# A four-layer decoder kernel: the last layer's experts in groups of four, and layer 2's causal masks added on TensorE

## The chip, the cores and the metric

The kernel runs on one core of one Trainium2 chip. The metric is the device time of one execution in microseconds (us), taken as the median over runs; lower is better. The core has five engines with queues of their own that meet through semaphores: TensorE (PE, matrix products into PSUM; its weight loads are shown as PEld), VectorE (DVE), ScalarE (ACT), GpSimd (POOL) and SyncE (SP), which in this kernel issues nearly all DMAs.

## The reference, cut to what matters

Four layers work one after the other on x of shape (4, 512, 128), each as self-attention, cross-attention to a context of 154 rows, and a feed-forward part, each followed by a residual and a layer norm. Two of the twelve parts matter here. The causal attention of layer 2 has 16 heads of 64, and keys and values are one projection; the last layer's feed-forward part is a mixture of one shared and seven routed experts with 352 inner values each.

```python
# layer 2, attention: a key after its query is masked; scale 1/sqrt(128), keys times 1 + k_weights
logits = jnp.where(mask, logits, jnp.asarray(-1000000.0, logits.dtype))
a = jax.nn.softmax(logits, axis=-1)
y = jnp.einsum("bhij,bhjv->bhiv", a, kv)          # then y @ w_o

# last layer, feed-forward
def _expert(x, wg, wu, wd):
    return jax.nn.silu(x @ wg) * (x @ wu) @ wd
shared_out = _expert(x, shared_gate, shared_up, shared_down)
probs = jax.nn.sigmoid(x @ Wr * routing_bias)
scores, idx = jax.lax.top_k(probs, TOPK)          # TOPK = 2
scores = scores / scores.sum(-1, keepdims=True)
for e in range(n_exp):                            # 7 routed experts
    combined = combined + _expert(xf, routed_gate[e], routed_up[e], routed_down[e]) * weights[:, e:e + 1]
return shared_out + combined.reshape(b, s, d)
```

Every expert is computed for every row, and the two chosen ones get a weight that isn't zero.

## The kernel before

The twelve parts are Python generators that emit instructions piece by piece. The order on each engine is the order in which the pieces are emitted, written out by hand; the scheduler does not reorder. A part has a first phase, which is interleaved with the end of the part before it by a pattern of letters (ORDER), a main phase, and a tail. An Agenda holds small pieces that are due at a given step (normalising a finished batch, routing the next). The work goes batch by batch, 512 rows at a time, kept transposed (features on the 128 partitions) as `xT`.

**Layer 2's attention (`l2_attn`, with the class `Causal`).** A unit is one batch and two heads; there are 4 x 8 = 32. Heads lie in partitions 0 to 63 and 64 to 127. The scores of a unit are a triangle of query tiles of 128: query tile qt meets qt + 1 key tiles. They are computed in three parts, `PARTS`: part 0 is query tile 3 (512 keys), part 1 is query tiles 2 and 0 (384 and 128 keys), part 2 is query tile 1 (256 keys), each for both heads. `scores` (L1137) puts the scores in a PSUM buffer `scc`. `maxima` (L1153) runs one custom DVE instruction for each query tile and head, which adds the bf16 mask tile `cmaskb`, turns the sign, writes the scores back to PSUM, and gives the negative maximum. `exps` (L1161) runs the exponential on ACT with that maximum as bias and also sums the rows; `norm` divides, with the reciprocal on DVE (L1167) and the product on POOL (L1170). `turned` (L1186) transposes the probabilities of the unit on PE into `ptc`, which ACT or DVE copies out (L1522, L1533, L1547), and `products` (L1199) multiplies by the values.

`step(i)` of `l2_attn` interleaves three units: queries and keys of unit i + 2 (`psqk`, L1471) and its values (`psv`, transposes of the keys, L1481), scores of unit i + 1, transposes and products of unit i, and the output projection of unit i - 1 (`ypo`, L1492). Eight times a step a PSUM buffer of two banks is taken, from a ring of three in fixed turn: scores 0, transposes 0, queries and keys, scores 1, transposes 1, scores 2, values, transposes 2. Each of these must wait until the one three turns earlier has been read. When a projection for the next part of the layer (`ps_proj`, L400) comes between, the turn moves on by one. Layer 1's feed-forward part uses the same class.

**The last layer's experts (`l3_ffn`).** For each batch and expert there are three chunks of inner values: 128, 128 and 96. `gated` (L1935) makes two products, gate and up, into a pair of PSUM banks `psgu` (or `psguy` and `psguv`), ACT makes the silu (L1937), and DVE the product into the tile `hT` (L1938). `down` (L1946) multiplies the three chunks of an expert by its down weights, into `ype`, and DVE adds it, with the routing weight, to `ys` (L1952, L1958). `chunk(q)` issues chunk q, and behind every second chunk of an expert the down product of the expert before it:

```python
            if c == 1 and q > NCH:
                before = q // NCH - 1
                down(*divmod(before, NE))
```

There are 4 batches x 8 experts x 3 chunks = 96 chunks. After the last one comes the last down product, then the layer norm of the last batch and its store.

The functions that the change touches, with the line numbers of the profile:

Of the kernel before, what the change touches and what calls it, by code (L numbers as in the profile page):

```python
# [21 lines left out]
P = 128  # L22
# [62 lines left out]
    return out.reshape(P, P)  # L85


def _rope_tables():
    freq = np.exp(np.arange(0, D, 2, dtype=np.float32) * np.float32(-np.log(10000.0) / D))
    ang = np.arange(S, dtype=np.float32)[:, None] * freq[None, :]  # L90
    return _fold(np.cos(ang).astype(np.float32)), _fold(np.sin(ang).astype(np.float32))


def _layer_params(name, p):

    if name == "L0_attn":
        cos, sin = _rope_tables()
        return dict(
            cos=cos, sin=sin,
            wq=_heads(p["Wq"].T), wk=_heads(p["Wk"].T), bq=_head_bias(p["bq"]), bk=_head_bias(p["bk"]),  # L100
            wv=p["Wv"].T, bv=_rows(p["bv"]), wo=p["Wo"].T, bo=_rows(p["bo"]),
        )
    if name.endswith("xattn"):
        out = dict(wq=_heads(p["Wq"].T), wk=_heads(p["Wk"].T), wv=p["Wv"].T)
        if "bq" in p:
            out |= dict(bq=_head_bias(p["bq"]), bk=_head_bias(p["bk"]), bv=_rows(p["bv"]))
        if "Wo" in p:
            out |= dict(wo=p["Wo"].T)
        if "bo" in p:
            out |= dict(bo=_rows(p["bo"]))  # L110
        if "gamma" in p:
            out |= dict(gamma=_rows(p["gamma"]), beta=_rows(p["beta"]))
        return out
    if name == "L0_ffn":
        return dict(
            w1=p["w1_w"].T, w2=p["w2_w"].T, s1=_cols(p["w1_s"]), s2=_cols(p["w2_s"]),
            h1=_fold(p["h1_w"].T), h1s=_cols(p["h1_s"]), h2=_fold(p["h2_w"].T), h2s=_cols(p["h2_s"]),
            w3=_fold(p["w3_w"].T), s3=_rows(p["w3_s"]),
        )
    if name == "L1_attn":  # L120
        wx = np.zeros((2 * P, P), np.float32)
        for at in (0, 64, 96):
            wx[:, at : at + 32] = p["W_x"][:, 8:]
        wx[:, 32:40] = p["W_x"][:, :8]
        wdt = np.zeros((P, 2 * P), np.float32)
        wdt[32:40] = p["W_dt"]
        return dict(
            w_in=p["W_in"], cwr=_rows(p["conv_w"].T), cb=_cols(p["conv_b"]), wx=_fold(wx), wdt=wdt,
            bdt=_cols(p["b_dt"]), alog=_fold(p["A_log"]), dd=_cols(p["D"]), wout=_fold(p["W_out"]),
        )  # L130
    if name == "L1_ffn":
        ve = p["value_experts"].transpose(2, 1, 0, 3).reshape(P, -1)
        oe = p["output_experts"].reshape(8, 4, 2, 64, P).transpose(2, 3, 1, 0, 4).reshape(P, -1)
        return dict(wq=p["w_q"], wk=p["w_k"], wg=p["w_gate"], ve=ve, oe=oe)
    if name in ("L1_ffn", "L2_attn"):
        return dict(wq=p["w_q"], wkv=p["w_kv"], kw=_cols(p["k_weights"]), wo=_fold(p["w_o"]))
    if name == "L2_ffn":
        return dict(
            dwk=p["dw_kernel"].reshape(P, 3), dwb=_cols(p["dw_bias"]), pw=p["pw_w"].T, pwb=_cols(p["pw_b"]),
            rw=p["router_w"].T, rb=_rows(p["router_b"]),  # L140
            ew=p["expert_w"].transpose(2, 0, 1).reshape(P, -1), eb=_rows(p["expert_b"]),
            ow=p["out_w"].T, ob=_rows(p["out_b"]), nw=_rows(p["norm_w"]),
            dn=p["ff_down_w"].T, dnb=_tall(p["ff_down_b"].reshape(-1, 1)), up=_tall(p["ff_up_w"].T),
            upb=_rows(p["ff_up_b"]),
        )
    if name == "L3_attn":
        return dict(
            wd=p["W_down"], wq=_heads(_block_diag(p["toqueries"])), wk=_heads(_block_diag(p["tokeys"])),
            wv=_block_diag(p["tovalues"]), wo=p["W_unify"], bo=_rows(p["b_unify"]),
        )  # L150
    if name == "L3_ffn":
        gate = np.concatenate([p["shared_gate"][None], p["routed_gate"]]).transpose(1, 0, 2).reshape(P, -1)
        up = np.concatenate([p["shared_up"][None], p["routed_up"]]).transpose(1, 0, 2).reshape(P, -1)
        dn = np.concatenate([p["shared_down"][None], p["routed_down"]])
        full = np.zeros((8, 3 * P, P), dn.dtype)
        full[:, : dn.shape[1]] = dn
        dn = full.reshape(8, 3, P, P).transpose(2, 0, 1, 3).reshape(P, -1)
        return dict(wr=p["Wr"], rb=_rows(p["routing_bias"]), gate=gate, up=up, dn=dn)
    raise KeyError(name)
# [15 lines left out]
def decoder_kernel(ctx: ExitStack, tc: tile.TileContext, x, ctxT, mask1, mask3, packs, offsets, out, layers):  # L175
# [936 lines left out]
    class Causal:  # L1112
# [4 lines left out]
        KEYS = (((0, 0),), ((1, 0), (3, 384)), ((2, 0),))  # L1117
        WIDTH = (512, 512, 256)

        def __init__(self, pool, room):  # L1120
            self.ap, self.room, self.work = pool, room, None

            self.mask = pool.tile([P, S], BF16, name="cmaskb", bufs=1)
            nc.gpsimd.memset(self.mask[:, : S - P], 0.0)
            make_causal_mask(nc, self.mask[:, S - P :], MASKED)
            self.nm = {}
            self.pr = {}
            self.pT = {}

        def scores(self, u, part, q, k):  # L1130

            sc = psum2("scc")
            for i, (qt, at) in enumerate(self.PARTS[part]):
                n = (qt + 1) * P
                for r in range(2):
                    rows = slice(64 * r, 64 * r + 64)
                    nc.tensor.matmul(  # L1137
                        sc[:, r, at : at + n], lhsT=q[rows, qt * P : n], rhs=k[rows, :n], start=(i == 0), stop=True,
                        skip_group_check=True,
                    )  # L1140
            nt = len(self.PARTS[part])
            nm = small.tile([P, 2, 2], F32, tag=f"nm{part}", name="nm")
            zs = small.tile([P, 2, 2], F32, tag=f"zs{part}", name="zs")
# [3 lines left out]
            def maxima():  # L1147

                for i, (qt, at) in enumerate(self.PARTS[part]):
                    n = (qt + 1) * P  # L1150
                    for r in range(2):
                        of = sc[:, r, at : at + n]
                        nc.vector.tensor_tensor_reduce(  # L1153
# [3 lines left out]
            def exps():  # L1157
                for i, (qt, at) in enumerate(self.PARTS[part]):
                    to = at + (qt + 1) * P
                    for r in range(2):  # L1160
                        nc.scalar.activation(  # L1161
                            pr[:, r, at:to], sc[:, r, at:to], AF.Exp, bias=nm[:, i, r : r + 1], scale=-1.0,
                            accum_out=zs[:, i, r : r + 1],
                        )

# [39 lines left out]
    def l1_ffn(w, cur, new, last, room):  # L1205
        NH, NE, DH, NC = 8, 8, 64, 4
        units = B * NC
        keep, pool = room.take("keep"), room.take("early")
        causal = Causal(pool, room)
        made, gates, yTs, oTs, gTs, waiting = {}, {}, {}, {}, {}, []  # L1210
        agenda = Agenda()
        state_x, state_T = cur["x"], cur["xT"]
# [240 lines left out]
    def l2_attn(w, cur, new, last, room):  # L1453
# [4 lines left out]

        nc.vector.tensor_scalar(kw1, w["kw"], 1.0, D ** -0.5, ALU.add, ALU.mult)
        wo = w["wo"].rearrange("p (c d) -> p c d", c=NC)  # L1460
        causal = Causal(pool, room)
        made, ypo, oTs = {}, {}, {}
        agenda = Agenda()
        state_x, state_T = cur["x"], cur["xT"]
# [420 lines left out]

    def l3_ffn(w, cur, new, last, room):

        NE, HID, NCH = 8, 352, 3
        keep = room.take("keep")
        dn = w["dn"].rearrange("p (e c d) -> p e c d", e=NE, c=NCH)  # L1890
        xs, xT = cur["x"], cur["xT"]
        weight, hidden, ys_of = {}, {}, {}
        agenda = Agenda()

        def routed(b):
# [31 lines left out]
        def gated(b, e, c):  # L1927
            src = xT[:, b, :]
            if c == 0:
                hidden[b, e] = keep.tile([P, NCH, S], F32, tag="hT", name="hT")  # L1930
            n = min(P, HID - c * P)
            at = e * HID + c * P
            ps = psum_pair("psgu")
            for r, wt in enumerate((w["gate"], w["up"])):
                nc.tensor.matmul(ps[r][:n], lhsT=wt[:, at : at + n], rhs=src, start=True, stop=True)  # L1935
            sg = keep.tile([P, S], F32, tag="sg", name="sg")
            nc.scalar.activation(sg[:n], ps[0][:n], AF.Silu)  # L1937
            nc.vector.tensor_tensor(hidden[b, e][:n, c, :], sg[:n], ps[1][:n], ALU.mult)  # L1938

        def down(b, e):  # L1940
            hT = hidden.pop((b, e))
            yp = psum_a("ype")
            for t in range(NT):
                for c in range(NCH):
                    n = min(P, HID - c * P)
                    nc.tensor.matmul(  # L1946
                        yp[:, t * P : (t + 1) * P], lhsT=hT[:n, c, t * P : (t + 1) * P], rhs=dn[:n, e, c, :],
                        start=(c == 0), stop=(c == NCH - 1),
                    )
            if e == 0:  # L1950
# [6 lines left out]
            for t in range(NT):  # L1957
                nc.vector.scalar_tensor_tensor(  # L1958
                    ys[:, t, :], yp[:, t * P : (t + 1) * P], weight[b][:, t, e - 1 : e], ys[:, t, :], ALU.mult, ALU.add
                )  # L1960

        def chunk(q):
            b, r = divmod(q, NE * NCH)
            e, c = divmod(r, NCH)
            if q < steps:
                gated(b, e, c)
            if c == 1 and q > NCH:
                before = q // NCH - 1
                down(*divmod(before, NE))
                if before % NE == NE - 1:  # L1970
                    agenda.add(q + 1, finish_pieces(before // NE, ys_of.pop(before // NE), new, last, split=True))
            agenda.run(q)

        steps = B * NE * NCH
        gated(0, 0, 0)
        yield PIECE
        routed(0)
# [6 lines left out]
                yield PIECE  # L1984
        yield READY
        for b in range(1, B):
            agenda.add(b * NE * NCH - 8, [lambda b=b: routed(b), lambda b=b: chosen(b)])
        for q in range(6, steps + 1):
            chunk(q)
            yield PIECE  # L1990
# [421 lines left out]
```

## Time and profile before

| | us |
|---|---|
| median of 3 runs | 2703.14 |
| lowest and highest | 2700.03, 2704.36 |
| the profiled execution, whole | 2705.39 |
| its span, first to last instruction | 2703.4 |

| engine | busy us | share of the span |
|---|---|---|
| PE | 2410.7 | 89% |
| PEld (weight loads, overlap PE) | 1161.6 | 43% |
| DVE | 1754.2 | 65% |
| ACT | 1247.0 | 46% |
| POOL | 1056.1 | 39% |

Layer 2's attention has its main phase from about 1452 to 1851 us of the span, the last layer's experts from about 2433 us to the end. In the profile's rows a group is given as line, engine, operation, output and inputs with the program's names, shapes (partitions x elements, or for PE rows x columns of the weights, then the moving operand), count, and busy time and mean duration. A row of a timeline begins with the start and the time until the group's end; what stands in brackets is the idle time before it and what released it. A matmul with f32 operands shows as two records, so counts of f32 matmuls are twice those in the code. The ends of matmuls are modelled, and neighbours seem to overlap by some hundredths of a microsecond; distances between starts are the safer measure.

### The profile page before, as it was taken

How to read it: one execution, taken by the hardware profiler on the slowest of the kernel's cores; microseconds unless marked ns; L12 is line 12 of the kernel's file. 1: busy time of each engine (PE TensorE's matmuls, PEld its weight loads, DVE VectorE, ACT ScalarE, POOL GpSimd, SP SyncE). 2: the span in 40 equal slices, each digit the busy share in tenths (PEclk: the TensorE clock that was granted, in tenths of full speed). 3: DMA queues.
4: the chain of work that ended last, by engine and by line, in shares of the span. 5: the costliest groups of instructions: out<-in, count | busy, mean ns of one | idle time of the engine just before them, and what ended most of it. 6: DMA issues, size and time to landing. Idle time of an engine off the chain costs nothing.

```text
span 2703.4 us, 37772 instructions
## 1 busy us (share of the span) xinstructions
PE 2410.7 (89%) x13974; PEld 1161.6 (43%) x13994; DVE 1754.2 (65%) x3484; ACT 1247.0 (46%) x2525; POOL 1056.1 (39%) x1376
## 2 busy tenths in 40 slices
PE   5898889978877989999999999997988999999998
PEld 1233334433334434444444555554455233446665
DVE  6796951288896665555556666666756887664444
ACT  3676432377652434333333455453543787443221
POOL 2342520166675336556542444443445343310000
PEclk9998999989998999999999999998998999999999
DMA  5421310000002400000000000002102241400000
GB/s 152 119 79 57 101 35 0 0 0 0 0 16 80 142 7 1 0 1 1 1 1 1 15 12 1 13 13 83 39 1 59 77 115 23 139 24 1 4 5 8
DMA packets 75560, 96.39 MB, mean 36 GB/s; under 512 B 23664, under 2 KB 62320, under 8 KB 75376
## 3 DMA queue, kind: packets, MB, share of 16 engines
q1 hardware_dynamic: 74224, 92.14, 11.7%
q8 instruction: 110, 1.80, 0.3%
q10 hardware_dynamic: 1152, 1.84, 0.2%
q14 instruction: 74, 0.61, 0.1%
HBM read 63.92 MB, written 33.49 MB: 36 GB/s over the span
## 4 chain that ended last, share of the span: by engine, by line
PE 62%; DVE 16%; ACT 9%; POOL 5%; issue 4%; DMA 2%; SPq 1%; POOLq 0%; DVEq 0%; ACTq 0%
PE psgu L1935 4%; PE psve L1289 4%; PE av L709 4%; PE yT L1332 3%; PE scc L1137 3%; PE ype L1946 3%; ACT pr L1161 3%; PE psh L1624 3%; DVE scc L1153 3%; PE avc L1199 3%; PE ptc L1186 3%; DVE top L967 2%; PE sc L670 2%; PE avx L995 2%; DVE top L674 2%
## 5 line engine op out<-in xcount | busy, mean ns | idle before, releaser
L1170 POOL TENSOR_TENSOR pr<-pr,zs 128x1024 f32<-128x1024 f32 x192 | 237.4, 1254 | 246.6 <-DVE zs L1167 232.4
L674 DVE TENSOR_REDUCE top<-sc 128x2 f32<-128x1024 f32 x256 | 300.8, 1216 | 46.8 <-PE sc L670 43.0
L695 ACT ACTIVATE pT<-st 128x512 f32<-128x512 f32 x512 | 276.1, 597 | 89.0 <-PE st L686 85.8
L1161 ACT ACTIVATE pr<-scc,nm 128x256 f32<-128x256 f32 (+3 forms) x384 | 199.0, 530 | 198.2 <-DVE zs L1167 78.3
L1153 DVE CUSTOM_DVE_ANT_0 scc<-scc,cmaskb 128x256 f32<-128x256 f32 (+3 forms) x384 | 191.5, 499 | 131.4 <-PE scc L1137 112.6
L967 DVE TENSOR_REDUCE top<-scx 128x4 f32<-128x616 f32 x256 | 192.1, 794 | 88.1 <-PE scx L954 77.2
L973 ACT ACTIVATE pTx<-stx 128x512 f32<-128x512 f32 x256 | 139.3, 596 | 202.8 <-PE scx L954 135.5
L2143 POOL TENSOR_TENSOR hh<-hh,cs 128x1024 f32<-128x1024 f32 x64 | 149.4, 2355 | 74.0 <-DVE hh L2139 50.1
L709 PE MATMUL av<-pT,vbuf 128*32 128x256 f32 x2048 | 162.8, 393 | 8.4 <-ACT avs L509 8.4
L492 POOL CAST nmP<-top 128x16 bf16<-128x16 f32 x96 | 25.6, 267 | 363.7 <-DVE top L967 202.5
L1294 DVE TENSOR_TENSOR vtmp<-psve,gm 128x1024 f32<-128x1024 f32 x64 | 78.3, 1224 | 133.2 <-PE psve L1289 133.1
L337 POOL TENSOR_TENSOR rsf<-mvf,eps 128x4 f32<-128x4 f32 x48 | 9.9, 206 | 393.7 <-DVE mvf L335 392.6
L1137 PE MATMUL scc<-k,q 64*128 64x512 f32 (+3 forms) x768 | 142.5, 469 | 10.8 <-ACT pr L1161 6.2
L1186 PE MATMUL ptc<-ident,pr 128*128 128x128 f32 x960 | 138.4, 282 | 10.3 <-ACT pT L1533 5.7
L2139 DVE TENSOR_TENSOR_SCAN hh<-da,pb 128x1024 f32<-128x1024 f32 x64 | 142.6, 2270 | 0.0
L1289 PE MATMUL psve<-w_L_ffn,xT 128*128 128x512 f32 x256 | 125.7, 615 | 17.4 <-ACT pr L1161 11.9
L670 PE MATMUL sc<-kP,qP 64*128 64x512 bf16 x512 | 106.3, 414 | 35.1 <-DMA qP<-far_q 16.6
L1299 POOL TENSOR_TENSOR vtmp<-vtmp 128x512 f32<-128x512 f32 x60 | 76.0, 1267 | 153.9 <-DVE vtmp L1294 133.6
L2152 PE MATMUL acc<-hh,ident 128*128 128x512 f32 x256 | 132.5, 644 | 3.1 <-DVE yt L2161 1.9
L1199 PE MATMUL avc<-pT,v 128*64 128x512 f32 (+3 forms) x768 | 131.2, 449 | 0.8 <-DVE pT L1522 0.5
L1186 PEld LDWEIGHTS ptc<-ident,pr 128*128 128x128 f32 x960 | 103.4, 141 | 55.1 <-issue 13.9
L1332 PE MATMUL yT<-gT,w_L_ffn 128*128 128x512 f32 x256 | 122.9, 603 | 0.0
(418 smaller groups left out, 5044.4 us busy)
## 6 DMA issues: line engine op xcount, KB each, us to landing
qP<-far_q SPq DMA_DIRECT2D x24, 768.0 KB, 6.3
w_L_ffn<-in_L_ffn SPq DMA_DIRECT2D x24, 512.0 KB, 6.5
far_q<-part SPq DMA_DIRECT2D x44, 192.0 KB, 2.8
qP<-far_q SPq DMA_DIRECT2D x24, 256.0 KB, 4.1
far_q<-part SPq DMA_DIRECT2D x44, 128.0 KB, 2.4
kP<-far_k SPq DMA_DIRECT2D x7, 768.0 KB, 5.3
kP<-far_kc SPq DMA_DIRECT2D x16, 231.0 KB, 4.5
w_L_attn<-in_L_attn SPq DMA_DIRECT2D x6, 512.0 KB, 6.6
```

What stands on the lines that cost most here:

```text
L674: return lambda: nc.vector.tensor_reduce(top[:, qt, 2 * gp : 2 * gp + 2], sc, AX.X, ALU.max, negate=True)
L695: nc.scalar.activation(pT, st, AF.Exp)
L709: nc.tensor.matmul(m["av"][32 * g : 32 * g + 32, part], lhsT=m["v"][:, kt, 4 * j + g, :], rhs=weights_of[s, g][:, part], start=(kt == 0 an ...
L967: nc.vector.tensor_reduce(ops.maxima(a)[:, 2 * qp : 2 * qp + 2, 2 * gp : 2 * gp + 2].rearrange("p i r -> p r i"), sc, AX.X, ALU.max, negat ...
L1137: nc.tensor.matmul(sc[:, r, at : at + n], lhsT=q[rows, qt * P : n], rhs=k[rows, :n], start=(i == 0), stop=True, skip_group_check=True,)
L1153: nc.vector.tensor_tensor_reduce(of, of, self.mask[:, S - n :], -1.0, 3.0e38, ALU.add, ALU.min, nm[:, i, r : r + 1])
L1161: nc.scalar.activation(pr[:, r, at:to], sc[:, r, at:to], AF.Exp, bias=nm[:, i, r : r + 1], scale=-1.0, accum_out=zs[:, i, r : r + 1],)
L1170: nc.gpsimd.tensor_tensor(pr[:, :, at : at + n], pr[:, :, at : at + n], zs[:, i, :, None].to_broadcast([P, 2, n]), ALU.mult)
L1186: nc.tensor.transpose(pt[:, r, to : to + P], self.pr[u, p][:, r, lo : lo + P], ident)
L1199: nc.tensor.matmul(av[64 * r : 64 * r + 64, kt * P :], lhsT=v[:, kt, 64 * r : 64 * r + 64], rhs=self.pT[u, part][:, r, at : at + n], start ...
L1289: nc.tensor.matmul(ps[:, r, :], lhsT=src[:, t * P : (t + 1) * P], rhs=w["ve"][:, h * 512 : (h + 1) * 512], start=True, stop=True,)
L1332: nc.tensor.matmul(yTs[b], lhsT=oe[:, c, e, :], rhs=gT[:, i, :], start=(c == 0 and e == 0), stop=(c == NC - 1 and e == NE - 1),)
```

## The change

Two independent edits.

*Experts by fours.* Experts are taken in groups of four (0 to 3 and 4 to 7). The gate and up weights are laid out anew on the host: the third chunk of each of the first three experts of a group gets, behind its own 96 columns, 32 of the last 96 columns of the fourth expert. So the third chunk of the first three is full, and the fourth has only two chunks of its own; a batch has 22 chunks instead of 24. The fourth expert's last 96 inner values come out in partitions 96 to 127 of three `hT` tiles; a DMA on SP's queue for each of the three (32 partitions x 512 values, 64 KB) joins them in a new tile `third`, partitions 0 to 95, and the fourth expert's down product reads its third chunk there. The list `chunks` takes the place of the division of q, and the down product that is due waits in a list.

*Masks on PE.* With `by_pe` set, as layer 2 does, `scores` adds the mask of the diagonal tile by a bf16 product of the identity with the last 128 columns of the mask tile, into the same PSUM buffer, once for each query tile and head (eight times in a unit). `maxima` is then one DVE reduction for each query tile over both heads (four in a unit), which doesn't write the scores back, and the exponential's scale is 1.0 instead of -1.0. Layer 1 passes False and keeps its instructions.

```diff
+def _by_fours(w):
+    w = np.asarray(w)
+    parts = []
+    for g in range(0, 8, 4):
+        for i in range(3):
+            parts += [w[g + i], w[g + 3, :, 256 + 32 * i : 288 + 32 * i]]
+        parts.append(w[g + 3, :, :256])
+    return np.concatenate(parts, axis=1)
...
             # Causal.scores
-                        sc[:, r, at : at + n], lhsT=q[rows, qt * P : n], rhs=k[rows, :n], start=(i == 0), stop=True,
+                        sc[:, r, at : at + n], lhsT=q[rows, qt * P : n], rhs=k[rows, :n], start=(i == 0), stop=not self.by_pe,
                         skip_group_check=True,
                     )
+            if self.by_pe:
+                for qt, at in self.PARTS[part]:
+                    for r in range(2):
+                        nc.tensor.matmul(
+                            sc[:, r, at + qt * P : at + (qt + 1) * P], lhsT=identb, rhs=self.mask[:, S - P :],
+                            start=False, stop=True, skip_group_check=True,
+                        )
...
             # maxima
+                    if self.by_pe:
+                        nc.vector.tensor_reduce(nm[:, i, :], sc[:, :, at : at + n], AX.X, ALU.max, negate=True)
+                        continue
...
             # exps
-                            pr[:, r, at:to], sc[:, r, at:to], AF.Exp, bias=nm[:, i, r : r + 1], scale=-1.0,
+                            pr[:, r, at:to], sc[:, r, at:to], AF.Exp, bias=nm[:, i, r : r + 1],
+                            scale=1.0 if self.by_pe else -1.0,
...
             # l3_ffn, gated
-            n = min(P, HID - c * P)
-            at = e * HID + c * P
+            i = e % 4
+            at = e // 4 * 4 * HID + i * NCH * P + c * P
             ps = psum_pair("psgu")
             for r, wt in enumerate((w["gate"], w["up"])):
-                nc.tensor.matmul(ps[r][:n], lhsT=wt[:, at : at + n], rhs=src, start=True, stop=True)
+                nc.tensor.matmul(ps[r], lhsT=wt[:, at : at + P], rhs=src, start=True, stop=True)
             sg = keep.tile([P, S], F32, tag="sg", name="sg")
-            nc.scalar.activation(sg[:n], ps[0][:n], AF.Silu)
-            nc.vector.tensor_tensor(hidden[b, e][:n, c, :], sg[:n], ps[1][:n], ALU.mult)
+            nc.scalar.activation(sg, ps[0], AF.Silu)
+            nc.vector.tensor_tensor(hidden[b, e][:, c, :], sg, ps[1], ALU.mult)
+            if c == 2:
+                if i == 0:
+                    third[b, e // 4] = keep.tile([P, S], F32, tag="third", name="third")
+                nc.sync.dma_start(third[b, e // 4][32 * i : 32 * i + 32, :], hidden[b, e][96:, 2, :])
...
             # down
             hT = hidden.pop((b, e))
+            rest = third.pop((b, e // 4)) if e % 4 == 3 else hT[:, 2, :]
...
-                    n = min(P, HID - c * P)
+                    n, of = (P, hT[:, c, :]) if c < 2 else (HID - 2 * P, rest)
...
+        chunks = [(b, e, c) for b in range(B) for e in range(NE) for c in range(2 if e % 4 == 3 else NCH)]
+        steps, waiting = len(chunks), []
+
         def chunk(q):
-            b, r = divmod(q, NE * NCH)
-            e, c = divmod(r, NCH)
+            b, e, c = chunks[q] if q < steps else (B, 0, q - steps)
             if q < steps:
                 gated(b, e, c)
-            if c == 1 and q > NCH:
-                before = q // NCH - 1
-                down(*divmod(before, NE))
...
+            if c == 1 and waiting:
+                before = waiting.pop(0)
+                down(*before)
...
+            if c == 1:
+                waiting.append((b, e))
             agenda.run(q)
```

More of the change, by code (lines that the diff above doesn't have):

```diff
@@ L151, in _layer_params @@
     if name == "L3_ffn":
-        gate = np.concatenate([p["shared_gate"][None], p["routed_gate"]]).transpose(1, 0, 2).reshape(P, -1)
-        up = np.concatenate([p["shared_up"][None], p["routed_up"]]).transpose(1, 0, 2).reshape(P, -1)
+        gate = _by_fours(np.concatenate([p["shared_gate"][None], p["routed_gate"]]))
+        up = _by_fours(np.concatenate([p["shared_up"][None], p["routed_up"]]))
         dn = np.concatenate([p["shared_down"][None], p["routed_down"]])
@@ L1118, in decoder_kernel, with __init__ @@
         WIDTH = (512, 512, 256)
-        def __init__(self, pool, room):
-            self.ap, self.room, self.work = pool, room, None
+        def __init__(self, pool, room, by_pe):
+            self.ap, self.room, self.work, self.by_pe = pool, room, None, by_pe
             self.mask = pool.tile([P, S], BF16, name="cmaskb", bufs=1)
@@ L1208, in l1_ffn @@
         keep, pool = room.take("keep"), room.take("early")
-        causal = Causal(pool, room)
+        causal = Causal(pool, room, False)
         made, gates, yTs, oTs, gTs, waiting = {}, {}, {}, {}, {}, []
@@ L1460, in l2_attn @@
         wo = w["wo"].rearrange("p (c d) -> p c d", c=NC)
-        causal = Causal(pool, room)
+        causal = Causal(pool, room, True)
         made, ypo, oTs = {}, {}, {}
@@ L1891, in l3_ffn @@
         xs, xT = cur["x"], cur["xT"]
-        weight, hidden, ys_of = {}, {}, {}
+        weight, hidden, ys_of, third = {}, {}, {}, {}
         agenda = Agenda()
@@ L1944, in down @@
                 for c in range(NCH):
-                    n = min(P, HID - c * P)
+                    n, of = (P, hT[:, c, :]) if c < 2 else (HID - 2 * P, rest)
                     nc.tensor.matmul(
-                        yp[:, t * P : (t + 1) * P], lhsT=hT[:n, c, t * P : (t + 1) * P], rhs=dn[:n, e, c, :],
+                        yp[:, t * P : (t + 1) * P], lhsT=of[:n, t * P : (t + 1) * P], rhs=dn[:n, e, c, :],
                         start=(c == 0), stop=(c == NCH - 1),
@@ L1960, in down @@
                 )
+        chunks = [(b, e, c) for b in range(B) for e in range(NE) for c in range(2 if e % 4 == 3 else NCH)]
+        steps, waiting = len(chunks), []
         def chunk(q):
-            b, r = divmod(q, NE * NCH)
-            e, c = divmod(r, NCH)
+            b, e, c = chunks[q] if q < steps else (B, 0, q - steps)
             if q < steps:
                 gated(b, e, c)
-            if c == 1 and q > NCH:
-                before = q // NCH - 1
-                down(*divmod(before, NE))
-                if before % NE == NE - 1:
-                    agenda.add(q + 1, finish_pieces(before // NE, ys_of.pop(before // NE), new, last, split=True))
+            if c == 1 and waiting:
+                before = waiting.pop(0)
+                down(*before)
+                if before[1] == NE - 1:
+                    agenda.add(q + 1, finish_pieces(before[0], ys_of.pop(before[0]), new, last, split=True))
+            if c == 1:
+                waiting.append((b, e))
             agenda.run(q)
-        steps = B * NE * NCH
         gated(0, 0, 0)
@@ L1986, in l3_ffn @@
         for b in range(1, B):
-            agenda.add(b * NE * NCH - 8, [lambda b=b: routed(b), lambda b=b: chosen(b)])
+            agenda.add(b * steps // B - 8, [lambda b=b: routed(b), lambda b=b: chosen(b)])
         for q in range(6, steps + 1):
```

## The prediction

> **What bounds the kernel now.** I first read the engine table: PE is busy for 2410.7 of 2703.4 us, so I looked at the two stages that the change touches, and asked in each whether PE ever waits. The windows view (length, then busy time of PE, PEld, DVE, ACT and POOL, then granted clock) shows the last layer's experts in a stretch of 60 us:
>
> ```profile
> 2480.00:2540.00 60.00, 60.00 (x289) 38.30 (x288) 28.95 (x83) 16.12 (x26) 1.21 (x2) 1.00 0.02 5
> ```
>
> PE never rests there and DVE is busy for half of it. The timeline of PE gives the prices (start, time until the end of the group, count; a matmul in f32 appears as two records, and ends are modelled, so I use distances between starts):
>
> ```profile
> 2675.27 3.60 PE L1935 MATMUL psgu<-xT,w_L_ffn 128*128 128x512 f32 x8
> 2678.70 2.84 PE L1946 MATMUL ype<-w_L_ffn,hT 128*128 128x128 f32 x24
> 2681.38 1.02 PE L1935 MATMUL psguy<-xT,w_L_ffn 128*96 128x512 f32 x2
> ...
> 2690.93 0.61 PE L1946 MATMUL ype<-w_L_ffn,hT 128*128 128x128 f32 x4
> 2691.93 2.50 PE L1946 MATMUL ype<-w_L_ffn,hT 96*128 96x128 f32 x20 [0.40 <-DVE hT L1938]
> ```
>
> Eight records, two chunks, take 3.43 us to the next start: 1.72 us a chunk; the down product of an expert takes 2.68. The chunk with 96 columns (128*96) costs the same, because its 512 moving columns are the same.
>
> Layer 2's attention is different. Its unit repeats every 12.33 us (two psqk starts) and PE waits in it:
>
> ```profile
> 1618.21 1.88 PE L1471 MATMUL psqk<-xT,w_L_attn 128*128 128x512 f32 x4
> 1620.02 1.14 PE L1137 MATMUL scc<-k,q 64*128 64x384 f32 x8
> 1621.09 1.09 PE L1186 MATMUL ptc<-ident,pr 128*128 128x128 f32 x8
> 1622.11 1.08 PE L1199 MATMUL avc<-pT,v 128*64 128x512 f32 x4
> 1623.12 1.16 PE L1492 MATMUL ypo<-w_L_attn,oT 128*128 128x128 f32 x8
> 1624.21 0.70 PE L1137 MATMUL scc<-k,q 64*128 64x256 f32 x4
> 1625.46 0.66 PE L1481 MATMUL psv<-ident,k 128*128 128x128 f32 x4 [0.55 <-ACT pr L1161]
> 1626.37 0.66 PE L1186 MATMUL ptc<-ident,pr 128*128 128x128 f32 x4 [0.25 <-ACT pT L1533]
> ```
>
> The scores of part 1 (1620.02) go to DVE for mask and maximum, then to ACT for four exponentials, and only when these are read does the ring of three PSUM buffers give psv its place; ptc then waits for the ACT copy behind them. Without the waits scc to psv would take about 0.63 (its 0.70 less the 0.07 by which neighbours overlap) instead of 1.25, and psv to ptc 0.49, as at 1612.08, instead of 0.91. With 0.05 for the restart that is 1.09 us of 12.33: PE's own work is 11.24. The chain of part 1 on DVE and ACT:
>
> ```profile
> 1621.32 0.57 DVE L1153 CUSTOM_DVE_ANT_0 scc<-scc,cmaskb 128x384 f32<-128x384 f32 x1 [0.43 <-PE scc L1137]
> ```
>
> ```profile
> 1623.48 0.58 ACT L1161 ACTIVATE pr<-scc,nm 128x384 f32<-128x384 f32 x1 [1.98 <-DVE zs L1167]
> ```
>
> From DVE's first mask instruction to the first exponential: 2.16 us, eight DVE instructions and a reciprocal.
>
> **The change, part by part.** *Experts by fours.* Each batch has 22 chunks instead of 24, so eight chunks go: 8 x 1.72 = 13.8 us of PE in a stage where PE never waits. Their eight silus (0.60 each) and products (0.69) on ACT and DVE go too, worth nothing, since both lie under PE. The other chunks keep their price (128 columns against 96, shown above). At the end the last expert's down product today waits for its third chunk: 1.00 us from 2690.93 to 2691.93 where four such records take 0.45. Afterwards the down product of expert 6 (2.68 us) lies between the last chunk and it, longer than silu and product (1.3): another 0.5 saved. Sum -14.3.
>
> It adds 24 DMAs of 64 KB on SP, whose queue has only four output stores in this stage (0.38 us each to issue); each waits for a DVE product, and an output store queued behind it is late by at most that product and one issue. PE's down product for the fourth expert is the only reader; behind it on PE stand the next gate and up products, and behind those ACT and DVE. No row shows an SBUF to SBUF copy; the nearest is far_q<-part with 64.0 KB, 2.1 us to landing, and the slowest of this size is far_k<-part, 3.7 us. A copy that was not there cannot gain, so the bounds are nothing and what exceeds the cover. The cover is four chunks and a down product on PE, 6.9 + 2.7, less 1.4 for silu and product: 8.1 us; in the very last group two chunks fewer, 4.7 us. I take zero; with a copy of 6 us the last join alone would stop PE, for 1.3. The buffer that the copy reads is written again two experts later, some 8 us on.
>
> *Masks on PE.* Per unit eight bf16 matmuls of 128 columns come in (2, 4 and 2 by part). Nearest row:
>
> ```profile
> L503 PE MATMUL pmx<-identb,nmP 128*128 128x128 bf16 x768 | 63.4, 229 | 10.2 <-POOL nmP L495 10.2
> ```
>
> Its 229 ns is the latency of one; eight in a row take 0.46 us to the next f32 group (2397.93 to 2398.39), 58 ns each. Low bound: 0.16 a unit, if the mask also swallows the 0.10 that today's step from 64-row scores to 128-row transposes costs (1.07 to ptc here, 0.97 to the 64-row psg in layer 1). High bound: unpipelined, 8 x 0.229 = 1.83. I take 0.46. The Trainium skill ("TensorE: Matmul & The Clock Gate", section "Back-to-back issue gap") speaks against the change: with a weight load before every matmul it gives about 81 ns at 128 columns, 0.65 a unit. The row has such loads and shows 58, so I keep 0.46; with 81 the sum below would be 6 us worse.
>
> On DVE, eight mask instructions (697, 566, 432, 299 ns twice each, and 141 ns for reading out each) become four reductions. The form exists as L674, 1216 ns for 1024 elements, and L967, 794 ns for 616: 1.034 ns an element plus 157. So 1216, 951, 422, 687 ns: 3.28 us instead of 5.12. The skill ("VectorE: DVE Perf Modes", section "Rules for kernel authors") calls the reduction the slowest DVE operation and advises to restructure. Here the removed instruction streams at (697 - 299)/384 = 1.036 ns an element, the same; the saving is in instructions. By that rule alone I would give part 1 no saving, and the masks would lose all of their 0.46.
>
> Only part 1's chain counts: 0.95 + 0.42 less 0.05 overlap, and 0.20 to the exponential as now: 1.52 instead of 2.16, but starting 4 x 0.058 = 0.23 later. With scores at 0: exponentials begin at 3.05 (now 3.46), end at 4.98, the copy ends at 5.88. PE, with 0.35 of masks before it, reaches psv at 5.17, so that wait goes, and ptc at 5.66, where 0.28 is left: what is late next is ACT's copy of part 1. Unit: 11.24 + 0.46 + 0.33 = 12.03, 0.30 less than 12.33. The unit after it, whose DVE starts 0.1 earlier, gives 0.45 the same way. Behind the longer score groups on PE queue transposes and products; part 0's exponentials, which free part 1's buffer, gain 0.33 on DVE and lose 0.12 on PE. POOL's division (5.0 us a unit) is done at about 9.3 after the scores, and its last reader comes at about 9.9: no new wait, but little left, and none at the batch ends, where PE already waits for POOL (0.74 and 0.34 at 1616.93). So of 32 units I count 30 at 0.30: -9. The exponential's other sign costs nothing; layer 1 keeps the old masks. POOL builds the mask tile as before, at the start of the stage.
>
> **Sum.** -14.3 - 9 = -23.3. The profiled execution took 2705.4 us around its span of 2703.4, and 2705.4 - 23.3 = 2682.1. It lies 2.2 above the median; against the median 2703.1 the forecast is 2679.8, rounded to 2680.
>
> **The rivals.**
> 1. *Experts as forecast, masks even.* PE takes up the masks, but ACT's copy or POOL's division keeps the unit at 12.3: for it, POOL waits at every batch end and 0.6 us of slack; against it, the 0.4 us that the chain of part 1 gets shorter. 2703.1 - 14.3 = 2689.
> 2. *Slower.* The masks do not pipeline between f32 neighbours, 0.229 each: 1.83 a unit less the 1.09 of waiting which this swallows is 0.74 x 32 = 24 us, and with the experts' -14.3 about 2713. It decides from 0.19 us a mask ((1.09 + 14.3/32)/8). For it: no row has a bf16 group just behind f32 scores in one accumulation. Against it: pmx stands between f32 groups at 58 ns.
> 3. *The join waits.* The copy lands later than its cover, so the fourth experts stop PE. Each of eight joins would have to wait 1.8 us to eat the 14.3, a copy of about 10 us; with half of that, 2687. Against it: 2.1 us at this size.
> 4. *All waits of layer 2 go.* 30 x 0.63 = 19 us instead of 9: 2670. Then PE would be full in both stages.
> That the change doesn't do what it says can be left aside: the chunk list has 88 entries by its own expression.
>
> **How the numbers follow.** Forecast 0.55, its own range 2674 to 2686; rival 1 0.23; rival 4 0.09; rival 3 0.05; rival 2 0.08. The range 2668 to 2694 takes in the forecast, rivals 1 and 4 and part of 3. A difference of 0.2% (5.4 us) is about what can be told from no change. Faster by more than that: forecast, 1, 4 and half of 3, 0.89; within it 0.04; slower 0.07.
>
> **What would show it.** In the changed profile, PE should have 4 x 22 chunks of psgu, 60.00 of 60.00 busy still, and no wait for a DMA at the fourth down product; the stage from the first psgu to the end shorter by 14. In layer 2 the psv wait on the exponentials should be gone, ptc should wait up to 0.3 for the ACT copy, two masks should lengthen scores by about 0.12 and four by 0.23, and the unit should be near 12.0. Mask groups at 0.15 us each or more, a unit at 12.3, or a DMA named as releaser of ype would make it wrong.

## The result, and the profile after

The changed kernel takes 2676.2 us (median of four runs, 2671.3 to 2676.7), the kernel before 2702.9 measured beside it: a ratio of 0.9903, with a 95% interval from 0.9889 to 0.9917. That is 26.8 us less, where 23.3 were forecast; 2676 lies in the range and 4 us from the predicted time. The profiled execution took 2676.1 us, with a span of 2674.3.

The experts, by the windows view (columns as before), are still a stage in which PE never rests:

```profile
2467.00:2527.00 60.00, 60.00 (x289) 38.93 (x289) 28.87 (x82) 15.83 (x26) 1.21 (x2) 1.00 0.05 12
```

so every chunk that is gone is 1.72 us gone. The timeline of PE at the end of the kernel shows the price of a chunk and what became of the last wait:

```profile
2658.60 1.88 PE L1962 MATMUL psgu<-xT,w_L_ffn 128*128 128x512 f32 x4
2660.31 3.29 PE L1978 MATMUL ype<-w_L_ffn,hT 128*128 128x128 f32 x28
2663.44 0.39 PE L1978 MATMUL ype<-w_L_ffn,third 96*128 96x128 f32 x2
2663.66 0.61 PE L1978 MATMUL ype<-w_L_ffn,hT 128*128 128x128 f32 x4
```

The chunk still takes 1.71. The 28 records are expert 6's down product and the beginning of expert 7's, with nothing in brackets between them: the wait of 0.40 for DVE that stood there before has gone. The rows with `third` are the joined chunk, and they too start without a wait. The view of that tile says how early the copies were (duration is the issue on SP's queue):

```profile
L1969 SPq DMA_DIRECT2D third<-hT x24: 507/507/558, 2431.0 to 2658.4; - x24
DMA to landing us min/median/max: 1.9/1.9/2.5
```

In layer 2, one unit of PE's timeline, which stands against the unit shown before:

```profile
1622.48 1.88 PE L1494 MATMUL psqk<-xT,w_L_attn 128*128 128x512 f32 x4
1624.29 1.14 PE L1149 MATMUL scc<-k,q 64*128 64x384 f32 x8
1625.36 0.40 PE L1156 MATMUL scc<-cmaskb,identb 128*128 128x128 bf16 x4
1625.60 1.04 PE L1209 MATMUL ptc<-ident,pr 128*128 128x128 f32 x8
...
1628.67 0.70 PE L1149 MATMUL scc<-k,q 64*128 64x256 f32 x4
1629.30 0.28 PE L1156 MATMUL scc<-cmaskb,identb 128*128 128x128 bf16 x2
1629.42 0.61 PE L1504 MATMUL psv<-ident,k 128*128 128x128 f32 x4
1630.09 0.66 PE L1209 MATMUL ptc<-ident,pr 128*128 128x128 f32 x4
...
1634.48 1.02 PE L1494 MATMUL psqk<-xT,w_L_attn 128*128 128x512 f32 x2
```

The unit is 12.00 us (1622.48 to 1634.48) where it was 12.33 (12.22 in some of the units beside it) and where the sum had 12.03. Four masks cost 0.24 from start to start, two cost 0.12 ahead of psv. The wait of psv for the exponentials is gone. From psv to ptc there are 0.67 us; nothing stands in brackets, but 0.45 is what this step takes where nothing is waited for (seen below), and ptc starts 0.05 after the end of ACT's copy of part 1's transposes:

```profile
1629.02 1.02 ACT L1556 COPY pT<-ptc 128x1024 f32<-128x1024 f32 x1
```

The chain that shortened, on DVE and then on ACT:

```profile
1625.80 1.29 DVE L1171 TENSOR_REDUCE nm<-scc 128x2 f32<-128x768 f32 x2 [0.64 <-PE scc L1156]
```

```profile
1627.20 0.58 ACT L1183 ACTIVATE pr<-scc,nm 128x384 f32<-128x384 f32 x1 [1.43 <-DVE zs L1190]
```

1.40 from the first reduction to the first exponential, where it was 2.16 and where 1.52 had been summed.

**Where the time went.** I put the stages side by side by starts of PE records: layer 2's attention from the last `yT` record of the part before it to the last `ypo`, the experts from the first `psgu` to the end of the span.

| kernel | layer 2's attention | experts |
|---|---|---|
| before | 401.6 | 270.1 |
| after | 392.0 | 253.6 |
| difference | -9.6 (forecast -9) | -16.5 (forecast -14.3) |

The length of layer 2's attention repeats well: 401.6 in both kernels here with the old masks on DVE alone, and within 0.1 of 392.0 in the four whose layer 2 is that of the change. So differences of some tenths in it can be told apart, which the times of whole executions don't allow.

The 2.2 us that the experts have too much are not the change's, as the second experiment shows. A further 3.4 us of the difference of the spans are there before layer 2 begins (the last `yT` at 1449.5 and at 1446.1), in instructions that are the same in both. In the profiles of the kernels here that leave layer 1 alone, the first `yT` starts anywhere from 1039.8 to 1044.9 us, which is not tied to what they change. So of the 26.8 us, some 24 are the two edits (9.6 + 14.3), and some 3 are of the kind by which single executions differ.

### The profile page after: what moved, and what is told of

Its sections match the earlier page's. It is cut to its first block, busy times and chain, and to the rows that moved or that the text cites. A ratio compares the mean times of both kernels' runs of the same rounds, so it can differ in the third digit from the quotient of the medians.

```text
span 2674.3 us, 37907 instructions
## 1 busy us (share of the span) xinstructions
PE 2413.6 (90%) x14198; PEld 1171.3 (44%) x14218; DVE 1708.0 (64%) x3092; ACT 1244.2 (47%) x2517; POOL 1056.5 (40%) x1376
## 4 chain that ended last, share of the span: by engine, by line
PE 65%; DVE 14%; ACT 8%; POOL 5%; issue 4%; DMA 2%; SPq 1%; POOLq 0%; DVEq 0%; ACTq 0%
PE av L721 4%; PE psgu L1962 4%; PE psve L1312 4%; PE scc L1149 4%; PE avc L1222 3%; PE yT L1355 3%; PE ype L1978 3%; PE ptc L1209 3%; PE psh L1647 3%; ACT pr L1183 3%; PE sc L682 2%; DVE top L979 2%; PE avx L1007 2%; PE psqk L1494 2%; PE st L698 2%
## 5 line engine op out<-in xcount | busy, mean ns | idle before, releaser
L1171 DVE TENSOR_REDUCE nm<-scc 128x2 f32<-128x1024 f32 (+3 forms) x128 | 102.4, 821 | 118.5 <-PE scc L1156 118.5
```

## The experiments

The theory is that of the prediction: the experts' gain is eight chunks of a PE that is never idle; the masks' gain is the shorter chain of part 1 on DVE and ACT, which gives PE back more waiting than the masks cost it. The main rivals: one edit alone does it; PE's time alone counts, or any work on PE hides; the joins cost something.

**The experts alone** (`experts_only`): `Causal(pool, room, False)` in layer 2.

```diff
         # l2_attn
-        causal = Causal(pool, room, True)
+        causal = Causal(pool, room, False)
```

> The experts by fours alone; layer 2 keeps its masks on DVE. Theory (two independent gains, each as forecast): 14.3 us below the kernel before, about 2689; up to 16 if the spell at half clock that the trace of before shows at the start of this stage (eight psgu records in 4.83 us instead of 3.43) stays away. Rival (the experts gave less than forecast and layer 2 more): 2695 or above. Rival (the joins do cost PE): a DMA as releaser of ype rows and 2692 or above.

2689.7 us (2687.4 to 2692.3) against 2703.8; ratio 0.9947, interval 0.9932 to 0.9962: 14.2 less. Layer 2's attention is 401.6, as before; the experts take 254.0.

**The masks alone** (`masks_only`): `l3_ffn` and the order of its weights as before.

> Layer 2's masks on PE alone; the experts keep 24 chunks a batch. Theory: PE takes 0.5 us of masks a unit and loses 1.1 us of waiting less some rest, so 9 to 10 us below the kernel before, about 2693, with a unit of 12.0. Rival (rival 1 of the prediction, masks even): within 3 us of 2703. The two kernels' gains should add up to that of the whole change, 26.8, within 3 us.

2692.7 (2688.0 to 2700.7) against 2703.8; ratio 0.9961, interval 0.9949 to 0.9972: 11.1 less. Layer 2's attention takes 392.0, as in the whole change. The two gains together are 25.3, within 1.5 of the whole. So the gains add up, as far as the runs can tell, and neither edit does it alone.

This run also has the experts of the kernel before, in a second execution: 267.9 us from the first psgu to the end, not 270.1. The difference shows in one row, first before, then here:

```profile
2438.85 5.00 PE L1935 MATMUL psgu<-xT,w_L_ffn 128*128 128x512 f32 x8
```

```profile
2429.53 3.60 PE L1958 MATMUL psgu<-xT,w_L_ffn 128*128 128x512 f32 x8
```

Two chunks took 5.00 instead of 3.60. The granted clock was 0.50 from 2438.24 to 2441.65 and 1.00 on both sides, where the changed kernel shows 1.00 in the same work. Half the clock for 3.41 us costs 1.7 of the 2.2 us; for the rest no cause is shown. With 267.9 as the base, the experts gained 14.3 (253.6) and 13.9 (254.0).

What brings such a spell can be read in part. From 1000 us on, the spells at half clock in each of the twelve traces start on a grid of 3.413 us. Where the step of the grid ahead of a spell was at full clock, PE stood idle in it for 1.36 us or more, and every such step with more than 1.82 us of idle PE was followed by a spell; in between, these traces show both. In the kernel before, PE's wait of 1.55 just ahead lies wholly in one step (2434.83 to 2438.24), and the spell follows; here a step ends in the middle of the same wait (at 2428.27, of 2427.49 to 2429.04), and the clock stayed at 1.00. The Trainium skill ("TensorE: Matmul & The Clock Gate", section "What's actually happening") tells of a gate that halves the clock after an idle window of about 3.4 us, with windows that run free. The length and the free running agree with these traces; but here a window of which less than half was idle was followed by a spell.

**Both masks** (`both_masks`): PE adds the mask, and DVE runs its old instruction too.

```diff
-                    if self.by_pe:
+                    if False:
                         nc.vector.tensor_reduce(nm[:, i, :], ...)
...
-                            scale=1.0 if self.by_pe else -1.0,
+                            scale=-1.0,
```

> The whole change, but layer 2's DVE work is left as it was before: the old mask instruction adds the mask a second time, one instruction for each head, with PE's masks in front. Theory (the gain comes from the shorter chain of part 1 on DVE and ACT, not from PE): that chain starts 0.23 later and is as long as before, so psv waits again; with part 0's two masks on top the unit is 12.6 to 12.8, layer 2 is 9 to 15 us slower than before the change and 18 to 25 slower than with it: about 2697. Rival (any work on PE hides in its waits): unit near 12.3, about 2687. Rival (the chain does not matter, PE is the bound with about 11.8 of own work): unit 12.0, about 2676.

2705.2 (2701.1 to 2709.8) against 2703.8; ratio 1.0004, interval 0.9995 to 1.0013. Layer 2's attention takes 418.4: 16.8 more than before the change, 26.4 more than with it. But this execution has a spell at half clock in the stage (0.50 from 1460.45 to 1463.87), and the stages compared with have none. From psv to psqk it took 6.87 there (1459.49 to 1466.36), and 5.30 in the next unit, so 1.6 us are the spell's. Without it the stage is 15.2 above before and 24.8 above the change, at the upper end of what I expected (9 to 15, and 18 to 25). On PE the wait stands where it stood:

```profile
1632.90 0.65 PE L1504 MATMUL psv<-ident,k 128*128 128x128 f32 x4 [0.49 <-ACT pr L1183]
1633.80 0.66 PE L1209 MATMUL ptc<-ident,pr 128*128 128x128 f32 x4 [0.25 <-ACT pT L1556]
```

The unit is 12.89. From part 1's scores to psv it is 5.78 instead of 5.44, 0.34 more; I had counted 0.23. Part 0's masks cost 0.22 ahead of `avc` (128*64); I had counted 0.12. So the masks on PE cost some 15 us while the chain is long, and the four reductions in place of eight mask instructions give back some 25. The gain of this edit comes from DVE; PE pays for it.

**Masks twice** (`masks_twice`):

```diff
-                for qt, at in self.PARTS[part]:
+                for qt, at in self.PARTS[part] * 2:
```

> The whole change with every mask product of layer 2 issued twice (16 a unit instead of 8). It measures the price of a mask on a PE that is the bound. Theory (58 ns each, as the pmx row): 8 x 0.058 x 32 = 15 us more than the change, less up to 5 where PE still waits for ACT's copy, about 2687 to 2691. Rival (the skill's 81 ns with weight loads): 21 us more, 2697. Rival (0.22 each, unpipelined): 56 us more, 2732.

2690.1 (2688.5 to 2691.2) against 2703.8; ratio 0.9946, interval 0.9929 to 0.9963: 13.9 more than the change. Eight mask products in a row:

```profile
1632.32 0.62 PE L1156 MATMUL scc<-cmaskb,identb 128*128 128x128 bf16 x8
1632.78 1.04 PE L1209 MATMUL ptc<-ident,pr 128*128 128x128 f32 x8
```

0.46 for eight against 0.24 for four: 55 ns each. All together the unit grows by 0.33, to 12.33, not by 8 x 0.055 = 0.44, because psv to ptc shrinks from 0.67 to 0.55: that much of it was waiting. In the stage it is 402.0 - 392.0 = 10.0; the rest of the 13.9 is not the masks', since the profiled execution has one spell at half clock more than the change's in each of two stages whose instructions are the same (from the first `yT` to the last 407.7 us instead of 405.6, the experts 255.3 instead of 253.6). The pmx row had the right price; 81 ns would have made 0.65.

**The joins left out** (`no_join`):

```diff
-            rest = third.pop((b, e // 4)) if e % 4 == 3 else hT[:, 2, :]
+            rest = hT[:, 0, :] if e % 4 == 3 else hT[:, 2, :]
```

and the DMAs and the tile are gone.

> The whole change without its DMA joins; the fourth expert's third chunk is read from its own first chunk instead, so that part of the experts is not computed. Theory (the copy of 1.9 us to landing lies wholly under PE's 8.1, or 4.7 at the end): the same time as the change within 2 us, about 2676. Rival (the 24 copies, or their queue, delay PE or DVE): 3 to 10 us less than the change.

2676.3 (2674.0 to 2677.9) against 2704.6; ratio 0.9898, interval 0.9883 to 0.9913. The experts take 253.6, as with the joins, so the joins cost nothing that can be seen.

**Layer 1 too** (`layer1_too`): `Causal(pool, room, True)` in `l1_ffn`.

> The whole change, with masks on PE in layer 1's feed-forward part as well (16 units of the same class). There PE waits only 19 us in some 380, nearly all of it at batch ends, so there is little waiting to give back. Theory (masks on PE pay only where PE waits for the chain behind the scores): PE pays 0.5 to 0.6 us a unit, 8 to 10 us, and gets back at most a third: 3 to 9 us more than the change, about 2682. Rival (the shorter DVE work pays wherever it is): 3 us or more less than the change.

2687.0 (2682.2 to 2688.3) against 2704.6; ratio 0.9940, interval 0.9923 to 0.9956: 10.8 more than the change; in the profile, from the first `yT` to the last, 412.8 instead of 405.6. The change's profile has two spells of 3.41 us at half clock in that stretch (from 1175.57 and 1397.43) and this one none; with 1.7 us for each, the 7.2 are 10.6, as by the runs. I expected 3 to 9, and was wrong on the price and on what could be given back. An undisturbed unit, from psqk to psqk, takes 28.00 us instead of 26.98, and here the masks cost this:

```profile
1261.07 1.14 PE L1149 MATMUL scc<-k,q 64*128 64x384 f32 x8
1262.14 0.40 PE L1156 MATMUL scc<-cmaskb,identb 128*128 128x128 bf16 x4
1262.47 0.60 PE L1334 MATMUL psg<-gateT,pick 64*128 64x512 bf16 x2
```

1.40 from scores to psg, where it took 0.97 without masks (1258.24 to 1259.21 in the change): 0.43 for four masks, nearly twice the price of layer 2. The scores and psg both use 64 rows of the array, and the mask, with 128, stands between them: scores to mask is 1.07 instead of the 0.97 from scores to psg, and mask to psg 0.33 instead of 0.24.

The expectation put PE's waits there nearly all at batch ends, and that was misread: in 9 of the 16 units of the change, `psve` waits for part 1's exponentials, mostly 1.27 us, more than the 0.55 of `psv` in layer 2 before. This wait stays, though DVE's work is shorter:

```profile
1234.63 1.29 DVE L1171 TENSOR_REDUCE nm<-scc 128x2 f32<-128x768 f32 x2
1236.24 1.01 ACT L1408 COPY pT<-ptc 128x1024 f32<-128x1024 f32 x1 [2.62 <-PE ptc L1209]
1237.15 0.59 ACT L1183 ACTIVATE pr<-scc,nm 128x384 f32<-128x384 f32 x1
1239.14 1.98 PE L1312 MATMUL psve<-w_L_ffn,xT 128*128 128x512 f32 x4 [1.27 <-ACT pr L1183]
```

In layer 1, ACT copies transposes (L1408) ahead of part 1's exponentials. The maxima are ready at 1235.92 and the exponentials start at 1237.15, behind that copy, which waits for PE; with the old masks, in the change, the maxima were ready at 1234.71 and the exponentials started at 1234.97, behind the same copy. So DVE is not the late link of this chain, and a faster DVE gives PE nothing back. The masks on PE pay where PE waits for this chain and DVE is what makes it late. (Layer 1 with that copy moved was not run.)

**The copy on DVE** (`copy_dve`): what was named as late next.

```diff
                 # l2_attn, step
-                nc.scalar.copy(*tB)
+                nc.vector.tensor_copy(*tB)
```

> The whole change, with the copy of part 1's transposes (pT) in layer 2 moved from ACT to DVE, which has time between part 1's and part 2's maxima. Theory (what is late next is ACT's copy behind the four exponentials; psv to ptc takes 0.67 us instead of 0.49): 0.12 to 0.18 a unit less, a unit of 11.85, 4 to 5 us less than the change: 2671 to 2672. Rival (PE is the bound already, the rest is a start after a switch): no difference. Rival (part 2's maxima are pushed back behind the copy): a wait of sccA on part 2's exponentials and a few us more than the change.

2673.2 (2670.2 to 2676.3) against 2704.6; ratio 0.9887, interval 0.9872 to 0.9902. The interval overlaps that of the change, but the stage is clear: 386.0 instead of 392.0, the unit 11.72 (1612.01 to 1623.73) or 11.79, as most are, instead of 12.00:

```profile
1618.83 0.29 PE L1156 MATMUL scc<-cmaskb,identb 128*128 128x128 bf16 x2
1618.95 0.61 PE L1504 MATMUL psv<-ident,k 128*128 128x128 f32 x4
1619.40 0.60 PE L1209 MATMUL ptc<-ident,pr 128*128 128x128 f32 x4
```

0.45 from psv to ptc: 0.22 of the 0.67 was waiting for ACT's copy, though the timeline showed no idle time for it. That is more than the 0.12 to 0.18 that I expected; the step after it gained 0.06 as well (ptc to avc, 0.59 in the change, 0.53 here).

**Part 0's mask back on DVE.** Three kernels: with the copy on DVE (`parts12_copy_dve`), without (`parts12`), and with the copy on DVE and only part 1's masks on PE (`part1_copy_dve`). Each has this edit wherever `by_pe` decides, with the parts named:

```diff
-            if self.by_pe:
+            if self.by_pe and part in (1, 2):
```

> As the kernel with the copy on DVE, and part 0 gets its mask by DVE again, so six masks a unit instead of eight are on PE. Theory: part 0's chain (maxima 1.55, exponentials 1.34) ends about 4.3 us after its scores begin, and the next scores that want its buffer come 4.4 after, so it does not matter, and PE saves 0.22 a unit: a unit of 11.55 to 11.65, 11 to 14 us less than the change: 2663. Rival (part 0's chain is the next to bind): scc waits for the exponentials of part 0, and the time is within 4 us of the change's.

2668.5 (2666.2 to 2671.2) against 2704.6; ratio 0.9870, interval 0.9855 to 0.9885; the stage 383.7. This is the best kernel here, 7.7 us below the change by the medians, and its interval lies wholly below that of the change (0.9889 to 0.9917). The unit is 11.57 (1617.41 to 1628.98), but at batch ends normalising holds DVE up (2.30 us of it, from 1576.10, stand ahead of part 0's mask at 1578.32), and part 0's exponentials are late:

```profile
PE scc L1149 <- ACT pr L1183: 4.3, 6, 1.1
```

(us waited in total, times, longest; the same row says 1.6, 7, 0.3 in the change.) So the slack that I claimed is there in the steady unit and not at the ends, and 383.7 falls short of what 0.43 a unit would give (392.0 - 30 x 0.43 = 379).

> The whole change, but part 0 gets its mask by DVE again; the copy stays on ACT. Theory (part 0's mask on PE costs 0.22 a unit and buys nothing, since part 0's chain has slack): a unit of 11.8, 5 to 7 us less than the change, about 2670. Rival (part 0's chain binds when the copy is on ACT, or PE's freed time is lost in the wait for ACT's copy): within 2 us of the change.

2674.6 (2671.3 to 2679.4) against 2701.2; ratio 0.9900, interval 0.9885 to 0.9915: by the runs no difference from the change. In the profile the stage is 389.0, 3.0 less, and the unit 11.78. The unit is as expected, the gain of the stage about half, for the same batch ends.

> As the best kernel so far (copy of part 1 on DVE, masks of parts 1 and 2 on PE), but part 2 too gets its mask by DVE, so that only part 1's four masks are on PE. Theory (each part's masks pay only where its chain binds; from the start of part 2's scores its exponentials end after about 3.0 us, and PE wants the buffer again after 2.7): PE saves 0.12 and waits about 0.3 for part 2's exponentials before the next scores: a unit of 11.7 to 11.85, 4 to 8 us more than the best kernel, about 2674. Rival (PE's own work alone counts): a unit of 11.45 and 4 us less than the best kernel.

2671.9 (2669.4 to 2673.8) against 2701.2; ratio 0.9886, interval 0.9869 to 0.9902, which overlaps that of the best kernel. Stage 386.9, unit 11.80, and the wait named beforehand, about 0.30, 15 times in the main phase:

```profile
1630.92 1.13 PE L1149 MATMUL scc<-k,q 64*128 64x512 f32 x4 [0.30 <-ACT pr L1183]
```

Part 2's two masks cost PE 0.12 a unit and save this wait, so they earn more than they cost: 386.9 against 383.7 in the stage. The kernel with the copy on DVE and no mask on PE was not run, so what the masks give beside that copy is shown for the parts only.

## Why the prediction was right, point by point

- *Eight chunks at 1.72.* Right in the price and in the cover: -14.3 forecast, -14.2 by the runs of the experts alone, -13.9 and -14.3 in the stage against the undisturbed 267.9. That a chunk of 96 columns costs the same holds in the rows of before, too (2681.38 to 2683.10, 1.72). The 0.5 at the end is in it: the wait of 0.40 is gone.
- *The joins at zero.* Right: 1.9 us to landing (2.1 was taken from the nearest row) against covers of 8.1 and 4.7, and the same 253.6 when they are left out. Rival 3 falls.
- *A mask at 58 ns.* Right: 55 to 60 in part 1 and ahead of psv. Rival 2, which needed 0.19, falls; so does the page's 81 for this case. Mis-sized: part 0's two masks cost 0.22 and not 0.12, since the term left out what stands behind them. The sum of the eight came out all the same (0.48 against 0.46), because the steps behind the other masks got shorter: 0.97 instead of 1.02 from ptc to avc, 0.45 instead of 0.49 from psv to ptc. That is luck.
- *DVE's reductions.* Right, a little too dear: 1.40 to the exponential, 1.52 in the sum. The reductions took the 1.29 that the rows above show, against 1.32, and the exponential started 0.11 behind them; the 0.20 that the sum takes "as now" is 0.10 in the rows of before (read-out to 1623.38, exponential at 1623.48). The advice of the page against reductions did not hold here, since the instruction that went was as slow by element and needed twice as many pieces, each with a read-out of 141 ns.
- *What is late next.* Right in kind: ACT's copy. It was put at 0.28 + 0.05 us and measured 0.22 + 0.06. The unit came out at 12.00 against 12.03: PE's own work 11.72 (the unit with the copy on DVE) against 11.70, the wait 0.28 in all against 0.33.
- *Thirty units at 0.30.* Right in sum, -9.6 against -9, but not unit by unit. From psqk to psqk the units inside a batch gained 0.21 to 0.46, most of them 0.21, 0.22 or 0.33; the first gained 0.82, and two at each batch's end, for which the sum had nothing, 0.31 to 0.59 and 0.13. That these make up for the units below 0.30 is luck.
- *POOL's division gives no new wait.* Right: PE waits 4.2 us for it in layer 2's main phase (4.0 before), all at batch ends. Rival 1 falls.
- *Whole time.* The forecast of 2680 was 4 us high, within what single executions of one kernel differ by.

## What to carry to other kernels

Moving work to the engine that is the bound can still pay, if it shortens a chain that this engine waits for at the link that makes it late: count the wait given back against the price, unit by unit, and only for the pieces whose chain binds. The same edit was worth -9.6 us in layer 2, where PE waited 1.1 us a unit for a chain that DVE made late, and cost some 10 in layer 1, where PE waited too (mostly 1.27 us, in 9 of 16 units) for the same exponentials, but these stood behind a copy on ACT; within layer 2 it was better kept to two parts of three. When a sum names what will be late next, that is also the next thing to change: the copy moved to DVE took another 6 us from the stage.

## What the runs showed of the hardware that I had not expected

A small product costs what its neighbours make of it: two bf16 masks of 128 columns took 0.12 us between scores and psv (128*128), 0.22 between scores and avc (128*64), and four took 0.24 in layer 2 but 0.43 between two products of 64 rows in layer 1. More of the same in a row add 55 ns each. And a wait of 0.22 us can be there with nothing in the brackets, since a PE group's modelled end reaches over it (psv's to 1630.03, ptc starts at 1630.09); the end of ACT's copy at 1630.04 and the distance of starts between two versions show it. Spells at half clock of 3.41 us fall in other places from one execution to the next and cost 1.6 to 1.7 us each, as much as some of the effects measured here, so a stage is compared only after a look at its granted clock.
